# Moving evictions, waits and loads between engines at the borders of a two-layer graph transformer

## The chip, the cores and the metric

The kernel runs on one core of a Trainium2 chip. The metric is the device time of one execution in microseconds (us); the kernel before was run three times, with a median of 1898.72 us. One further execution was recorded by the hardware profiler, and all profile lines come from that one. Engines are named as the profile names them: PE is TensorE (matrix multiply), PEld its weight load, DVE is VectorE, ACT is ScalarE, POOL is GpSimd, SP is SyncE. SP, ACT and POOL each have a queue from which DMAs are issued, in the order in which the program lists them; an engine carries out its own instructions in order too.

## The reference

Two identical layers of a graph transformer over N = 2708 tokens of width 512, with 8 heads of 64:

```
mask   = adj + eye(n)
q,k,v  = h @ Wq.T + bq,  h @ Wk.T + bk,  h @ Wv.T + bv
scores = q.k / sqrt(64), -1e9 where mask == 0
ctx    = softmax(scores) @ v                       (per head)
h1     = layer_norm(h + ctx @ Wo.T + bo)
h2     = layer_norm(h1 + relu(h1 @ W1.T + b1) @ W2.T + b2)   (hidden width 2048)
```

The adjacency matrix `adj` is 2708 x 2708 int32 with a few ones in each row, so that attention is a sum over a handful of neighbours.

## The kernel before

All arithmetic is in 32-bit floats. Tokens are cut into 22 tiles of 128 rows (`NT` = 22; the last has 20). The order of the work on every engine is the order in which the Python program emits it, written out by hand; the framework adds only the waits.

**Keys stage, layer 0** (`first`). For each tile `t`, PE makes the keys `k` (four matmul steps into a PSUM tile of tag "g", three buffers) and the values `v` (tag "f", three buffers). DVE adds the key bias and evicts `k` into `kvs` (L919); ACT evicts `v` (L921); ACT's queue then issues the write of the tile before into DRAM (`kv_d`, L923). Beside this `lists(t)` turns rows of the adjacency into a list of neighbours: SP's queue loads 128 rows of `adj` into `aj` (1354 KB, two buffers, L691), POOL adds the diagonal (L692), ACT writes a code of each entry (L696, two `code` buffers), and DVE finds the largest entries by MAX8 (L699, L703, L706). `LEAD` sets how many lists have been emitted at a tile: `while done < min(NT, 1 + LEAD * t)`. With `LEAD` = 1.3 the last list is emitted at t = 16. `counted()`, some 35 DVE instructions on how long the lists are, is emitted at the start of t = 21. `matrix(w, "Wq", ...)` is loaded by POOL's queue at t = `QT` = 6. `beside_keys` loads layer weights at t = 17, 20 and 21.

**Queries stage, layer 0** (`first_queries`). Each of 22 tiles is projected to `q` (tags "g" and "f" in turn). At t = 1 `ranked` sorts the tokens by the length of their lists (PE, then DVE); at t = 3 `inverted` makes `ident_i`, the order of the tokens, with which every later gather is addressed, and `last_keys` evicts the last tile's keys. At t = `OWN` = 7 PE turns three gathered tiles `xr`.

**Attention** (`attend`) is a generator: one step handles up to two neighbours of each of 128 tokens. POOL gathers their rows (L1068), DVE multiplies and reduces (L1105, L1111), ACT takes the exponential and weighs (L1124, L1131), DVE adds (L1137, L1144). `advance(x)` runs steps by a credit of x; `through(k)` runs all that block `k` still needs. The end of a tile's attention is `cx` (L1175).

**Blocks.** `attended` turns `cx`, fetches the residual rows `xb` (in layer 0 a gather by POOL, in layer 1 a load by SP), projects with Wo and normalises to `h`. `feed_forward` runs over f = 0 to 15 for each of 11 blocks of two tiles: `pf` (L1440), relu on ACT (L1451), second product `a` (L1413). In it, at f = 10 (12 for the very first block), the next block's `attended` begins.

**Border to layer 1.** `Layer.query` makes the queries of layer 1, evicts them on DVE (L1346), and `kept` writes them to `q_d` by SP's queue (L1357). Eight tiles' inputs are preloaded (`pool`); `queries` streams the others through three `zT` buffers, loaded by SP (L1332). `keys_values` turns the last block (ACT copies `zT`) and makes its keys and values.

```
            for _ in streamed:
                if len(got) < 2:
                    advance(0.6)
            through(0)
            early[n] = now.attended(blocks[0], got)
```

Of the kernel before, what the change touches and what calls it, by code (L numbers as in the profile page):

```python
# [18 lines left out]
P = 128  # L19
# [25 lines left out]
LEAD = 1.3  # L45
QT = 6
# [433 lines left out]
def by_edges(ctx: ExitStack, tc: tile.TileContext, x, xT, adj, layers, out, redo):  # L480
# [134 lines left out]
    def lists_of(pa):  # L615
# [69 lines left out]
        def lists(t):  # L685

            q0, r = t * P, size(t)
            aj = pa.tile([P, N], I32, tag="aj", name="aj")
            if len(full) > 1:
                kept()  # L690
            nc.sync.dma_start(out=aj[:r], in_=adj[q0 : q0 + r, :])  # L691
            nc.gpsimd.tensor_tensor(  # L692
                aj[:r, q0 : q0 + r], aj[:r, q0 : q0 + r], diag[:r, :r], ALU.add
            )
            code = codes[t % 2]
            nc.scalar.activation(halves(code, BF16, 1)[:r], aj[:r], AF.Square)  # L696
            tops = pa.tile([P, len(parts), 8], F32, tag="tops", name="tops", bufs=3)
            for k, (m, mw) in enumerate(parts):
                nc.vector.max(out=tops[:r, k, :], in_=code[:r, m : m + mw])  # L699
            full.append((t, tops))  # L700
            left = tops.rearrange("p k e -> p (k e)")
            for k in range(0, LIST, 8):
                nc.vector.max(out=top[:r, t, k : k + 8], in_=left[:r])  # L703
                if k + 8 < LIST:
                    cb = pa.tile([P, len(parts) * 8], F32, tag="cb", name="cb")
                    nc.vector.match_replace(  # L706
                        out=cb[:r],
                        in_to_replace=top[:r, t, k : k + 8],
                        in_values=left[:r],
                        imm_value=0.0,  # L710
                    )
                    left = cb
# [153 lines left out]
    def first(w, meanwhile):  # L866
# [41 lines left out]
        for t in range(NT):  # L908
            r = size(t)
            if t == NT - 1:  # L910
                counts = counted()
# [6 lines left out]
            if t < NT - 1:  # L918
                nc.vector.tensor_tensor(kv[:r, :DM], k[:r], bk[:r], ALU.add)  # L919
# [7 lines left out]
            while done < min(NT, 1 + LEAD * t):  # L927
                lists(done)
                done += 1
            meanwhile(t)  # L930
# [11 lines left out]
    def first_queries(bq, wq, counts, placing, pa, tokens, last_keys, meanwhile):  # L942
# [22 lines left out]
        for t in range(NT):  # L965
# [7 lines left out]
            if t == 3:  # L973
# [276 lines left out]
    class Layer:  # L1250
# [102 lines left out]
        def kept(self):  # L1353
            if self.due:
                g, qs = self.due
                r = size(g)
                nc.sync.dma_start(out=q_d[self.n][g * P : g * P + r, :], in_=qs[:r])  # L1357
            self.due = None

        def attended(self, block, got):  # L1360

            cTs, hs = [], []
            for g in block:
# [4 lines left out]
                xb = dn.tile([P, DM], F32, tag="row", name="xb", bufs=3)  # L1368
                fetch(self.n, xb, x if self.n == 0 else xb_d[self.n], g)
                cTs.append((g, r, cT, xb))  # L1370
            yield
            for g, r, cT, xb in cTs:
# [225 lines left out]
    def beside_keys(t):  # L1598

        if t == NT - 5:  # L1600
            now.load_first()
        if t > NT - 3:
            now.load_second(t + 2 - NT, temp)
            now.load_w1(t + 2 - NT, nc.gpsimd if t == NT - 2 else nc.sync)
            now.load_w2(t + 2 - NT)

    def beside_queries(t):

        if t < 2:
            now.load_w1(t + 2, nc.scalar)  # L1610
            now.load_w2(t + 2, nc.scalar)
# [19 lines left out]
    for n in range(NL):  # L1631
        last = n == NL - 1
        nxt = None if last else Layer(n + 1, layers[n + 1])
        if n > 0:
# [7 lines left out]
            while pool:  # L1642
                advance(0.6)
                now.query(*pool.pop(0))
            for _ in streamed:
                if len(got) < 2:
                    advance(0.6)
# [7 lines left out]
            finish(streamed)  # L1655
# [4 lines left out]
        turning = projecting = None  # L1660
        for k, block in enumerate(blocks):
# [4 lines left out]
            for f, zs in enumerate(now.feed_forward(block, hs, hT)):  # L1666
                if f == NFC:
                    break
                if f in (5, 6, 7, 8) and behind:
                    next(behind)  # L1670
                if more and f == 10 + 2 * (k + n == 0):
                    through(k + 1)
                    projecting = now.attended(blocks[k + 1], got)
# [122 lines left out]
```

## Time and profile before

| | |
|---|---|
| median of 3 runs | 1898.72 us (1898.07 to 1901.28) |
| profiled execution, its own time | 1895.18 us |
| its span, first to last instruction | 1893.4 us |
| PE busy | 1841.4 us, 97% |
| DVE busy | 1390.7 us, 73% |
| ACT busy | 932.1 us, 49% |
| POOL busy | 744.9 us, 39% |
| HBM traffic | 314.79 MB read, 50.65 MB written |

The span is what the trace covers; 1.8 us lie around it. Times inside the trace count from the span's start. PE being busy nearly throughout, time can only come from the places where it waits, or runs at half of its clock; these are few, and the stage in which each one lies matters more than the shares of the whole.

### The profile page before, as it was taken

The page shows a single profiled execution, that of the slowest core. Times are in us where ns is not written, and L with a number is a line of the kernel's source. Part 1 is how long each engine was busy: PE and PEld are TensorE (multiplying, and loading weights), DVE is VectorE, ACT ScalarE, POOL GpSimd, SP SyncE. Part 2 cuts the span into 40 slices and gives each one's busy share as a digit, 9 for nine tenths or more (in the row PEclk, how much of TensorE's full clock was granted, in tenths as well). Part 3 has the DMA queues.
Part 4 walks back from the last instruction along what each step waited for, and adds up shares of the span by engine and source line. Part 5 has one row for each costly group of instructions (what it writes and reads, how often), then busy time and mean ns, then how long its engine had stood idle before and what let it go on. Part 6 is the DMA issues. An engine that isn't in the chain of part 4 may idle for free. (4 is left out here: it accounts for less than half of the span.)

```text
span 1893.4 us, 20835 instructions
## 1 busy us (share of the span) xinstructions
PE 1841.4 (97%) x6172; PEld 1091.3 (58%) x6172; DVE 1390.7 (73%) x2181; ACT 932.1 (49%) x3218; POOL 744.9 (39%) x714
## 2 busy tenths in 40 slices
PE   8999999999999999999999998999999999999996
PEld 4434455665666656666565643566666666666663
DVE  6897668877777858678684165789898898888931
ACT  4651335555445555455543122556565575566520
POOL 2111655434444434434431041435454556355210
PEclk9999999999999999999999999999999999999998
DMA  8999967546545555553531775836454765465200
GB/s 314 348 314 289 356 208 239 194 145 228 178 158 170 172 195 172 183 184 118 194 134 52 252 276 202 288 119 238 161 198 164 244 228 179 145 217 189 84 11 9
DMA packets 133019, 366.91 MB, mean 194 GB/s; under 512 B 19290, under 2 KB 39082, under 8 KB 130188
## 3 DMA queue, kind: packets, MB, share of 16 engines
q0 software_dynamic: 69600, 248.45, 38.3%
q1 hardware_dynamic: 51652, 97.04, 15.0%
q10 hardware_dynamic: 11644, 20.00, 2.9%
q8 instruction: 50, 0.82, 0.2%
q14 instruction: 73, 0.60, 0.1%
HBM read 314.79 MB, written 50.65 MB: 193 GB/s over the span
## 5 line engine op out<-in xcount | busy, mean ns | idle before, releaser
L1440 PE MATMUL pf<-hT,w 128*128 128x256 f32 (+1 forms) x2816 | 632.8, 372 | 6.2 <-ACT hT L1246 4.6
L1440 PEld LDWEIGHTS pf<-hT,w 128*128 128x128 f32 x2816 | 518.4, 190 | 179.8 <-issue 98.0
L1068 POOL DMA_INDIRECT kv<-kv_d,listed x420 | 503.7, 1199 | 300.4 <-DVE acc L1144 126.6
L1413 PE MATMUL a<-w,ft 128*128 128x512 f32 x1312 | 611.1, 592 | 0.0
L1451 ACT ACTIVATE ft<-pf,b 128x256 f32<-128x256 f32 (+1 forms) x336 | 154.6, 462 | 452.8 <-PE pf L1440 437.0
L1413 PEld LDWEIGHTS a<-w,ft 128*128 128x128 f32 x1312 | 246.8, 190 | 187.4 <-issue 170.4
L1131 ACT ACTIVATE kv<-kv,p 128x64 f32<-128x64 f32 x1232 | 311.0, 335 | 5.0
L1231 POOL TENSOR_TENSOR rd<-va,mhalf 128x1 f32<-128x1 f32 (+1 forms) x88 | 81.2, 923 | 555.3 <-DVE va L1229 555.3
L1105 DVE TENSOR_TENSOR kv<-kv,q 128x1024 f32<-128x1024 f32 (+1 forms) x222 | 256.6, 1156 | 17.8 <-DMA q<-q_d,ident_i 11.5
L1111 DVE TENSOR_REDUCE sc<-kv 128x16 f32<-128x1024 f32 (+1 forms) x222 | 257.9, 1162 | 7.6
L1144 DVE TENSOR_TENSOR acc<-acc,kv 128x1024 f32<-128x1024 f32 (+2 forms) x178 | 205.2, 1153 | 68.3 <-ACT kv L1131 53.9
L1124 ACT ACTIVATE p<-sc,listed 128x8 f32<-128x8 f32 x420 | 103.7, 296 | 117.9 <-DVE sc L1111 87.0
L1137 DVE TENSOR_TENSOR kv<-kv,p 128x512 f32<-128x512 f32 (+1 forms) x178 | 122.8, 690 | 42.1 <-ACT p L1124 37.8
L587 PE MATMUL o<-wo,cT 128*128 128x512 f32 x336 | 148.1, 593 | 0.0
L587 PEld LDWEIGHTS o<-wo,cT 128*128 128x128 f32 x336 | 63.5, 190 | 80.9 <-issue 75.6
L1175 ACT ACTIVATE cx<-acc,su 128x64 f32<-128x64 f32 (+1 forms) x352 | 88.3, 333 | 18.2 <-issue 7.2
L696 ACT ACTIVATE code<-aj 128x2708 bf16<-128x2708 int32 (+1 forms) x22 | 73.2, 3327 | 48.0 <-POOL aj L692 48.0
L1235 DVE SCALAR_TENSOR_TENSOR h<-h,rd,ln_b 128x512 f32<-128x512 f32 (+1 forms) x88 | 66.1, 751 | 39.9 <-POOL rd L1231 39.9
L587 PE MATMUL k<-wk,xg 128*128 128x512 f32 x168 | 82.4, 636 | 12.0 <-DVE kvs L919 7.0
L699 DVE MAX8 tops<-code 128x8 f32<-128x247 f32 (+2 forms) x242 | 78.7, 400 | 17.8 <-ACT code L696 17.6
L1375 DVE TENSOR_TENSOR h<-o,xb 128x512 f32<-128x512 f32 (+1 forms) x44 | 30.2, 686 | 83.6 <-PE o L587 32.6
L1131 ACT ACTIVATE acc<-kv,p 128x64 f32<-128x64 f32 (+1 forms) x352 | 88.8, 334 | 1.4
(168 smaller groups left out, 1502.4 us busy)
## 6 DMA issues: line engine op xcount, KB each, us to landing
aj<-in_adj SPq DMA_DIRECT2D x21, 1354.0 KB
kv_d<-kvs ACTq DMA_DIRECT2D x21, 512.0 KB
xg<-in_xT SPq DMA_DIRECT2D x19, 512.0 KB
w<-in_W SPq DMA_DIRECT2D x19, 512.0 KB
kv<-kv_d,listed POOLq DMA_INDIRECT x420
w<-in_W ACTq DMA_DIRECT2D x12, 512.0 KB
q_d<-qs SPq DMA_DIRECT2D x22, 256.0 KB
zT_d<-zT SPq DMA_DIRECT2D x22, 256.0 KB
```

The source lines that it names most:

```text
L587: nc.tensor.matmul(o[:r], xs(c), wm[:, c, :], start=(c == 0), stop=(c == NC - 1))
L1068: return nc.gpsimd.indirect_dma_start(out=to, out_offset=None, in_=table[:, :], in_offset=bass.IndirectOffsetOnAxis(ap=s, axis=0), bounds_ ...
L1105: nc.vector.tensor_tensor(kv[:r, :c, :DM], kv[:r, :c, :DM], self.q[:r].unsqueeze(1).to_broadcast([r, c, DM]), ALU.mult,)
L1111: nc.vector.tensor_reduce(self.sc[:r, s0 : s0 + c, :], kv[:r, :c, :DM].rearrange("p s (h d) -> p s h d", d=DK), AX.X, ALU.add,)
L1124: nc.scalar.activation(p[:r, s, :], self.sc[:r, s, :], AF.Exp, bias=minus[:r, g, s : s + 1])
L1131: nc.scalar.activation(to[:, i, hd], kv[:r, i, DM + h * DK : DM + (h + 1) * DK], AF.Copy, scale=p[:r, s0 + i, h : h + 1],)
L1137: nc.vector.tensor_tensor(to[:, 0, :].rearrange("p (h d) -> p h d", d=DK), kv[:r, 0, DM:].rearrange("p (h d) -> p h d", d=DK), p[:r, s0, : ...
L1144: nc.vector.tensor_tensor(self.acc[:r, :c, :], self.acc[:r, :c, :], kv[:r, :c, DM:], ALU.add)
L1175: nc.scalar.activation(cx[:r, hd], self.acc[:r, 0, hd], AF.Copy, scale=self.su[:r, h : h + 1])
L1413: nc.tensor.matmul(a[:r], fts[f][:, c0 : c0 + r], self.w2[f // 2][:, f % 2, :], start=(f == 0), stop=(f == NFC - 1),)
L1440: nc.tensor.matmul(pf[:, :w], self.w1[f // 2][:, c, f % 2 * P : f % 2 * P + P], hT[:, c, :w], start=(c == 0), stop=(c == NC - 1),)
L1451: nc.scalar.activation(ft[:, :w], pf[:, :w], AF.Relu, bias=self.b1[:, f : f + 1])
```

## The change

The keys of tiles 0 to 20 are copied out of PSUM by ACT, and POOL then adds the bias in SBUF. Rows of `adj` are loaded, coded and released in two halves (four buffers of half the size, so the same memory). `LEAD` falls to 1.2, which emits the last list at t = 17, and `counted()` follows it directly. Wq is loaded at t = 16, the first layer weights at t = 19. Four pairs of W1 and W2 pieces are loaded by POOL's queue, where before one W1 piece was; two pairs came from ACT's queue. `inverted` and `last_keys` move from t = 3 to t = 4. In layer 0, the residual rows of the next block are gathered at f = 5 (7 in the first block), ahead of `attended`. In layer 1's opening the queries are written by ACT's queue (while `apart` holds), the attention steps are emitted at other places and with a credit of 0.65.

```diff
@@ -42,8 +42,8 @@
 CXB = 3
 AHEAD = 10
 XB, XBS = 256, 11
-LEAD = 1.3
-QT = 6
+LEAD = 1.2
+QT = 16
 OWN = 7
 LISTS = (6, 9, 11, 14, 15, 17, 18, 19, 20, 21)
 EARLY = 3
@@ -685,15 +685,23 @@
         def lists(t):
 
             q0, r = t * P, size(t)
-            aj = pa.tile([P, N], I32, tag="aj", name="aj")
             if len(full) > 1:
                 kept()
-            nc.sync.dma_start(out=aj[:r], in_=adj[q0 : q0 + r, :])
-            nc.gpsimd.tensor_tensor(
-                aj[:r, q0 : q0 + r], aj[:r, q0 : q0 + r], diag[:r, :r], ALU.add
-            )
             code = codes[t % 2]
-            nc.scalar.activation(halves(code, BF16, 1)[:r], aj[:r], AF.Square)
+            for n0, n1 in ((0, N // 2), (N // 2, N)):
+                aj = pa.tile([P, N - N // 2], I32, tag="aj", name="aj", bufs=4)
+                nc.sync.dma_start(out=aj[:r, : n1 - n0], in_=adj[q0 : q0 + r, n0:n1])
+                d0, d1 = max(q0, n0), min(q0 + r, n1)
+                if d0 < d1:
+                    nc.gpsimd.tensor_tensor(
+                        aj[:r, d0 - n0 : d1 - n0],
+                        aj[:r, d0 - n0 : d1 - n0],
+                        diag[:r, d0 - q0 : d1 - q0],
+                        ALU.add,
+                    )
+                nc.scalar.activation(
+                    halves(code, BF16, 1)[:r, n0:n1], aj[:r, : n1 - n0], AF.Square
+                )
             tops = pa.tile([P, len(parts), 8], F32, tag="tops", name="tops", bufs=3)
             for k, (m, mw) in enumerate(parts):
                 nc.vector.max(out=tops[:r, k, :], in_=code[:r, m : m + mw])
@@ -907,8 +915,6 @@
         done, before = 0, None
         for t in range(NT):
             r = size(t)
-            if t == NT - 1:
-                counts = counted()
             xs = tokens(t, 0)
             kv = wts.tile([P, 2 * DM], F32, tag=f"w2_{5 + t % 3}", name="kvs")
             k = project(xs, r, wk, "k")
@@ -916,7 +922,8 @@
                 finish(turning)
                 finish(turning_q)
             if t < NT - 1:
-                nc.vector.tensor_tensor(kv[:r, :DM], k[:r], bk[:r], ALU.add)
+                nc.scalar.copy(kv[:r, :DM], k[:r])
+                nc.gpsimd.tensor_tensor(kv[:r, :DM], kv[:r, :DM], bk[:r], ALU.add)
             v = project(xs, r, wv, "v", other=True)
             nc.scalar.copy(kv[:r, DM:], v[:r])
             if before:
@@ -927,6 +934,8 @@
             while done < min(NT, 1 + LEAD * t):
                 lists(done)
                 done += 1
+                if done == NT:
+                    counts = counted()
             meanwhile(t)
             if t == QT:
                 wq = matrix(w, "Wq", "wq", nc.gpsimd)
@@ -970,7 +979,7 @@
             if t == 1:
                 parts = ranked(*counts)
                 evicted(0, held, qs)
-            if t == 3:
+            if t == 4:
                 inverted(parts)
                 last_keys()
                 pa.__exit__(None, None, None)
@@ -1354,10 +1363,20 @@
             if self.due:
                 g, qs = self.due
                 r = size(g)
-                nc.sync.dma_start(out=q_d[self.n][g * P : g * P + r, :], in_=qs[:r])
+                by = nc.scalar if self.apart else nc.sync
+                by.dma_start(out=q_d[self.n][g * P : g * P + r, :], in_=qs[:r])
             self.due = None
 
-        def attended(self, block, got):
+        def residuals(self, block):
+
+            xbs = []
+            for g in block:
+                xb = dn.tile([P, DM], F32, tag="row", name="xb", bufs=3)
+                fetch(self.n, xb, x if self.n == 0 else xb_d[self.n], g)
+                xbs.append(xb)
+            return xbs
+
+        def attended(self, block, got, xbs=None):
 
             cTs, hs = [], []
             for g in block:
@@ -1365,11 +1384,10 @@
                 cx = got.pop(g)
                 cT = dn.tile([P, NC, P], F32, tag="cT", name="cT", bufs=3)
                 flip(cx, r, cT[:, :, :r], self.bv)
-                xb = dn.tile([P, DM], F32, tag="row", name="xb", bufs=3)
-                fetch(self.n, xb, x if self.n == 0 else xb_d[self.n], g)
-                cTs.append((g, r, cT, xb))
+                cTs.append((g, r, cT))
+            xbs = xbs or self.residuals(block)
             yield
-            for g, r, cT, xb in cTs:
+            for (g, r, cT), xb in zip(cTs, xbs):
                 o = project(lambda c: cT[:, c, :r], r, self.wo, "o")
                 h = dn.tile([P, DM], F32, tag="h", name="h", bufs=4)
                 nc.vector.tensor_tensor(h[:r], o[:r], xb[:r], ALU.add)
@@ -1597,18 +1615,18 @@
 
     def beside_keys(t):
 
-        if t == NT - 5:
+        if t == NT - 3:
             now.load_first()
         if t > NT - 3:
             now.load_second(t + 2 - NT, temp)
-            now.load_w1(t + 2 - NT, nc.gpsimd if t == NT - 2 else nc.sync)
-            now.load_w2(t + 2 - NT)
+            now.load_w1(t + 2 - NT, nc.gpsimd)
+            now.load_w2(t + 2 - NT, nc.gpsimd)
 
     def beside_queries(t):
 
         if t < 2:
-            now.load_w1(t + 2, nc.scalar)
-            now.load_w2(t + 2, nc.scalar)
+            now.load_w1(t + 2, nc.gpsimd)
+            now.load_w2(t + 2, nc.gpsimd)
         if t == 6:
             now.settle()
             now.load_w1(4, nc.scalar)
@@ -1640,11 +1658,12 @@
             next(ahead)
             next(streamed)
             while pool:
-                advance(0.6)
+                if len(pool) < 3:
+                    advance(0.65)
                 now.query(*pool.pop(0))
-            for _ in streamed:
-                if len(got) < 2:
-                    advance(0.6)
+            for i, _ in enumerate(streamed):
+                if len(got) < 2 or i < 6:
+                    advance(0.65)
             through(0)
             early[n] = now.attended(blocks[0], got)
             next(early[n])
@@ -1652,12 +1671,14 @@
             next(streamed)
             for _ in blocks[0]:
                 next(early[n])
-            finish(streamed)
+            for i, _ in enumerate(streamed):
+                if i < 3:
+                    advance(0.6)
             now.apart = False
             now.load_w2(NFC // 2 - 1)
         *_, hs = early[n]
         hT = now.turned(blocks[0], hs)
-        turning = projecting = None
+        turning = projecting = xbs = None
         for k, block in enumerate(blocks):
             more = k + 1 < NB
             asking = iter(())
@@ -1668,9 +1689,12 @@
                     break
                 if f in (5, 6, 7, 8) and behind:
                     next(behind)
+                if more and n == 0 and f == 5 + 2 * (k == 0):
+                    xbs = now.residuals(blocks[k + 1])
                 if more and f == 10 + 2 * (k + n == 0):
                     through(k + 1)
-                    projecting = now.attended(blocks[k + 1], got)
+                    projecting = now.attended(blocks[k + 1], got, xbs)
+                    xbs = None
                     next(projecting)
                 if more and f == 11 + 2 * (k + n == 0):
                     *_, hs_next = projecting
```

## What was predicted

> **What bounds the kernel now.** First the page's busy times and slices.
>
> ```profile
> PE 1841.4 (97%) x6172; PEld 1091.3 (58%) x6172; DVE 1390.7 (73%) x2181; ACT 932.1 (49%) x3218; POOL 744.9 (39%) x714
> ...
> PE   8999999999999999999999998999999999999996
> ...
> DMA  8999967546545555553531775836454765465200
> ```
>
> PE works nearly throughout, so only its gaps can be won. The first slices (keys) and those after 1100 us (border to layer 1) have full DMA queues. Second, PE's waits, longest first (total us, times, longest):
>
> ```profile
> PE k L587 <- DVE kvs L919: 7.0, 3, 3.9
> PE q L587 <- DMA zT<-zT_d: 7.0, 1, 7.0
> ...
> PE tp L1241 <- ACT cx L1175: 4.7, 3, 4.4
> ...
> PE tp L1241 <- DVE h L1235: 3.4, 2, 2.9
> ```
>
> Each is a place that this change touches: keys waiting for eviction, queries for their input, the next block for attention, and for its h. Third, the stretches around them (length, busy us and count of each engine, clock, DMA share, GB/s), and PE in order of time:
>
> ```profile
> 85.00:100.00 15.00, 12.34 (x26) 5.15 (x25) 13.18 (x48) 9.55 (x5) 1.89 (x6) 0.89 0.96 343
> ...
> 138.00:151.00 13.00, 9.15 (x18) 3.72 (x17) 11.83 (x42) 7.48 (x4) 3.96 (x9) 0.87 1.00 283
> ...
> 1139.00:1150.00 11.00, 4.03 (x6) 1.51 (x5) 10.11 (x14) 6.34 (x26) 0.00 (x0) 0.73 0.89 351
> ...
> 1227.00:1238.00 11.00, 6.39 (x21) 4.00 (x19) 10.76 (x14) 10.39 (x43) 2.72 (x2) 0.84 0.49 178
> ```
>
> ```profile
> 142.93 5.40 PE L587 MATMUL k<-wk,xg 128*128 128x512 f32 x8 [3.85 <-DVE kvs L919]
> ```
>
> A gap costs more than its wait: the eight matmuls behind this one took 5.40 us, elsewhere 3.60, since the granted clock fell. DVE is busy 11.83 of 13 us there: it is late with lists, and the keys' eviction stands behind them in its order.
>
> **The change, part by part.**
>
> *Keys by ACT and POOL, LEAD, halves.* Rows:
>
> ```profile
> L919 DVE TENSOR_TENSOR kvs<-k,bk 128x512 f32<-128x512 f32 x21 | 14.0, 672 | 6.0 <-PE k L587 6.0
> ...
> L692 POOL TENSOR_TENSOR aj<-aj,diag 128x128 int32<-128x128 int32 x21 | 9.5, 453 | 92.5 <-DMA aj<-in_adj 88.9 <-ACT kvs L921 3.6
> ...
> L692 POOL TENSOR_TENSOR aj<-aj,diag 20x20 int32<-20x20 int32 x1 | 0.2, 214 | 2.8 <-DMA aj<-in_adj 2.8
> ```
>
> DVE loses 21 x 0.67 = 14 us. ACT gains 21 copies at 0.56 (its copy of v) = 12 us, and the second start of 22 codes: a 2708-wide one takes 3.33 us, a 64-wide activation 0.33, so halves are some 1.8 us each, +0.26 a list, 6 us. By its two L692 shapes POOL pays 2.2 ns a column, so 1.3 us for 512, 27 us in all. The Trainium skill ("GPSIMD Engine Reference", Engine selection) speaks against this: two-input elementwise work belongs on VectorE, GpSimd being about half as fast. Taken as a chain, 0.56 + 1.3 - 0.67 = 1.2 us a tile would make it 25 us slower. I take the trace: POOL was busy 9.21 of the 72 us from 13 to 85, and only the write to DRAM, issued a tile later on ACT's queue, waits for the bias. Behind the bias on POOL stand the next list's diagonal and tops; their `aj` lands later than the key (POOL waited 91.7 us for it in all), so nobody is kept.
>
> What PE waits for is now ACT, which stands in order behind the codes, and these behind `aj`. Codes came every 6.0 us (the first began at 18.7, the last at 144.07, 21 between). With LEAD 1.2 list 21 belongs to t = 17. At the old pace its code ends near 147, and the key of tile 18 is evicted right behind it. Its buffer is wanted by tile 21: a tile takes PE 16 x 0.43 = 6.87 us, tile 1 began at 16.75, so tile 21 at 154. 7 us remain. DMA descriptors halve from 10832 to 5416 bytes: the trace's 10832-byte ones took 37.6 ns a KB, 4096-byte ones 38.8, so at most 3% (nearest row), 20% at its 1024-byte row. Early freeing pulls the other way. I take nothing. Then all waits for kvs go: 2.67 + 0.53 + 3.85 at 88, 118 and 143 us, and twice 5.40 - 3.60 of slow clock: **-10.7 us**.
>
> *Counting sooner* runs on a DVE with no key eviction waiting: nothing; it costs 9.5 us (162.8 to 172.2) that ended just ahead of its use and now end some 5 us ahead. *Wq at t = 16* is wanted at t = 22, 40 us on; *first weights at t = 19* a stage later; their four POOL issues (0.54 each) and five small SP ones leave the place where SP's queue held `aj` and `xg` loads, if anything a gain. *Weights by POOL*: seven more issues at 0.5 to 0.8 us, about 5 us, at 150 to 160 us, where POOL was nearly idle and the DMA queues had a hole (0.71 over 151:167). They leave SP and ACT queues that waited for nothing critical. Without that cover they'd delay the index gathers by up to 5 us; I take zero.
>
> *`inverted` one tile later.* Two costs. It takes its five POOL gathers and the last kv_d write along. `k` of the last tile now holds a "g" buffer while q of t = 4 wants one, so that it waits for q of t = 0, evicted behind `ranked`. From the first `ranked` matmul to that eviction took 9.8 us (174.24 to 184.04); PE's work between is 1.8 + 2 x 3.44: +1.2 us. Then only three queries, not four, lie between `ident_i` and the turning of `xr`. The third `xr` landed 14.1 us after `ident_i` (185.6 to 199.7) and cost a 1.0 us wait; with 3.44 us less cover: +2.6 (none if its transfer meets less traffic; 1.8 more if the clock falls, as it did behind waits of 2.67, 3.85, 6.97 and 4.40, not behind one of 2.9). Sum **+3.8 us**.
>
> *Residual rows sooner.* At 313 us two gathers were issued, and DVE waited 6.5 us for the first; then PE waited 2.9 for `h` and 0.6 for the copies behind. Five f-steps of 3.44 us earlier the 8 us transfer is covered: **-3.3 us** (idle PE in 327:338). The other waits for `xb` cost DVE only. In POOL's order two issues of 1.0 us now stand before some key gathers, once a block; the "row" buffers they take are free at f = 5, `turned_row` having ended at f = 4. Past the first block DVE has that slack: PE had no wait for it from 338 to 700.
>
> *Queries written by ACT.* The 7.0 us wait had its load issued at 1138.01, behind two writes that waited for DVE; the buffer had been free since 1132.6. From issue to landing it took 8.4 us, so it now lands at 1141 against a need at 1139.4: of 9.4 us (7.0, and 2.4 at the lower clock) 1.6 stay. But the same line puts the last two writes of layer 0 ahead of ACT's copies of the last block's zT: these started at 1098.79, the second query's eviction ended at 1100.27, plus an issue of 0.33: +1.9. Each later write makes ACT wait for an eviction that DVE does ahead of the scores which ACT's next exponential needs, so it adds nothing there (0.33 us an issue). Net **-5.9 us**. Attention allows it: with rows landing at 1121.8 + 1.9, six steps of 4.3 us (1.22 + 1.22 + 0.68 + 1.22) and ten evictions of 0.69 end at 1156.4, and PE, at 1108.5 + 1.9 + 14 x 3.44 + 1.6, asks at 1160; before it did at 1166.0.
>
> *Attention moved at the border.* Idle DVE time at 1166:1190 (10.86 busy of 24) takes about two steps, as the three new advances of 0.6 ask for: 8.6 us of lead for block 1, with their gathers at POOL, which issued only 8 in that stretch. The wait for cx at 1227 was 4.4, with slow clock 5.7: **-5.7 us**. If the lead isn't there it stays.
>
> Sum: -10.7 + 3.8 - 3.3 - 5.9 - 5.7 = -21.8. The profiled execution took 1895.18, span 1893.4, so 1873.4 for its like; the median of runs stands 3.5 higher, so 1877.
>
> **The rivals.**
>
> *A: attention sets the border.* PE arrives earlier, finds the same gathers (DMA share 1.02 over 1117:1147) and waits as long, in the first block or in a later one. DVE busy 434.65 of 500 us over 1250:1750 speaks for it, its idle time at 1166 against it. Without the last two gains: 1889.
>
> *B: slower; ACT becomes the bound of the keys.* One late half stops ACT, and with it keys, values and their writes. The 7 us of margin are gone at 6.36 us a list; beyond, each 0.1 us costs 2.1 us at the last list. Slower than before needs 22 us more, that is 7.4 us a list, DMA descriptors 23% dearer per byte. For it: DMA is 0.92 to 1.00 full, halves start off a row's boundary, ACT now carries 2 x 0.56 + 0.33 + 1.2 x 3.6 = 5.8 of each 6.87 us. Against: the 4096-byte row. At 7.7: 1905.
>
> *C: the change doesn't do what it says.* Lists are paced by DMA; PE finishes keys early and gives it back waiting for `ident_i`, and the border's loads stay late. Then 1898, no change. Against it: list 21 was coded at 147, yet counting started at 162.8, behind evictions.
>
> **How the numbers follow.** My case 0.60 (1867 to 1884: 9 less if the flips and border cost nothing, 7 more with the clock's fall and one step missing); A 0.20; B 0.14; C 0.06. The measurement tells 0.2%, 3.8 us, from no change. Faster is my case and A, 0.80; same 0.06; slower 0.14. The range leaves out B and the tail: 1866 to 1894.
>
> **What would show it.** Right: no PE wait for kvs, queries starting near 156.5 instead of 167.3; a wait of 3 to 4 us for xr near 189; no wait for h near 320; zT's wait under 2 us; no wait for cx in the first block of layer 1. Wrong: PE's k or v waiting for ACT's kvs, codes further apart than 6.3 us, the half-clock stretches returning, or DVE waiting for the kv gathers at the border.

## The result, and the profile after

The changed kernel takes 1873.12 us in the median (1872.13 to 1875.34, 4 runs), the kernel before in the same series 1899.72 (1898.07 to 1901.28, 4 runs): a ratio of 0.9862 [0.9845, 0.9879], 26.6 us less. The profiled executions are 1895.18 and 1872.77 us, 22.4 apart; what follows explains these 22.4.

The page of the kernel after, busy time, PE's slices and the DMA engines' slices:

```profile
PE 1834.5 (98%) x6172; PEld 1090.1 (58%) x6172; DVE 1378.4 (74%) x2160; ACT 941.9 (50%) x3261; POOL 778.7 (42%) x743
...
PE   8999899999999999999999999999999999999997
...
DMA  9999867646545455463541676836554664446300
```

DVE and ACT moved as the diff says: 21 fewer DVE instructions, 43 more on ACT (21 copies, 22 second halves). PE is 7 us less busy with the same 6172 matmuls, because fewer of them ran at half clock.

PE's waits in the kernel after (total us, times, longest):

```profile
PE tp L1250 <- DMA xr<-in_x,ident_i: 7.9, 2, 6.5
PE pf L1458 <- ACT hT L1255: 6.3, 4, 2.2
...
PE q L587 <- DMA zT<-zT_d: 1.8, 2, 1.4
PE k L582 <- ACT zT L1255: 1.3, 1, 1.3
PE q L587 <- DVE qs L959: 1.0, 1, 1.0
PE o L587 <- ACT cT L1255: 1.0, 1, 1.0
...
PE tp L1250 <- DVE h L1244: 0.6, 1, 0.6
```

The waits for `kvs` (7.0 us) and for `cx` (4.7) are gone, those for `zT` (7.0) and `h` (3.4) have shrunk to 1.8 and 0.6. Three came new: `qs` 1.0 and ACT's `zT` copies 1.3, foreseen in kind, and ACT's copies of `cT` 1.0, not foreseen. One grew beyond what was foreseen: PE now waits 7.9 us for `xr`, for which it waited 0.8 before:

```profile
PE tp L1241 <- DMA xr<-in_x,ident_i: 0.8, 1, 0.8
```

Three stretches of the kernel after (length, then busy us and count of PE, PEld, DVE, ACT, POOL, then clock, DMA share, GB/s). The first two are those of before, in the keys; the third is the turning of `xr`:

```profile
85.00:100.00 15.00, 15.00 (x37) 6.63 (x36) 11.40 (x41) 11.42 (x10) 3.33 (x7) 1.00 1.01 388
138.00:151.00 13.00, 13.00 (x32) 5.74 (x31) 12.09 (x49) 2.34 (x4) 5.61 (x8) 1.00 0.75 219
185.00:198.00 13.00, 5.12 (x17) 3.14 (x17) 2.77 (x6) 1.76 (x3) 10.19 (x10) 0.66 1.01 357
```

In the keys PE is full and at full clock, 13.00 of 13 us with 32 matmuls where 9.15 us with 18 stood before. DVE is nearly as full with its lists as it was (12.09 of 13 us in the second stretch), but PE no longer waits for it. In the third stretch PE works 5.12 of 13 us at a mean clock of 0.66, and the DMA engines are full.

Where the time went is best seen by following marks on PE, one start time after the other. The last column is what the prediction booked for the part since the mark above.

| mark on PE (or the end) | before | after | shift | since the mark above | predicted |
|---|---|---|---|---|---|
| queries start | 167.27 | 154.61 | -12.7 | -12.7 | -10.7 |
| own queries, behind the turning of `xr` | 200.27 | 196.97 | -3.3 | +9.4 | +3.8 |
| layer 0, first `pf` of block 0 | 267.11 | 264.64 | -2.5 | +0.8 | 0 |
| layer 0, first `pf` of block 1 | 336.50 | 330.43 | -6.1 | -3.6 | -3.3 |
| layer 1, first query | 1091.18 | 1084.16 | -7.0 | -0.9 | 0 |
| layer 1, first `pf` of block 0 | 1189.83 | 1179.65 | -10.2 | -3.2 | -5.9 |
| layer 1, first `pf` of block 1 | 1265.23 | 1248.96 | -16.3 | -6.1 | -5.7 |
| last matmul | 1875.63 | 1861.15 | -14.5 | +1.8 | 0 |
| end of the span | 1893.39 | 1871.04 | -22.3 | -7.9 | 0 |

Up to the last matmul the change won 14.5 us, not 21.8. The other 7.9 came behind it, where nothing was predicted. The total landed near the forecast because these two misses offset each other, which is luck.

Each column is one execution. In a second profiled execution of the changed kernel (`after_again` below) the own queries came +7.3 where this one has +9.4, the first `pf` of block 0 +1.9 (here +0.8), that of block 0 in layer 1 -1.7 (here -3.2); every other row agreed within 0.2 us. So those three rows are known to some 2 us, not to 0.1.

The end can be seen in the timeline. The last instruction that the kernel after has on POOL starts 5.25 us ahead of its end, that of the kernel before started at 1880.26, 13.1 us ahead of its end:

```profile
1865.79 1.05 POOL L1040 DMA_INDIRECT out<-h,ident_i  x1 [1.09 <-DVE h L1244]
```

What lies between is the drain of POOL that closes the program: 9.298 us in the records of the trace before, 1.867 after, with the same last DMA. By the trace's records of DMA packets its last packet is done 2.45 us after the issue begins before and 2.46 after, and in both the drain begins only then, so its length is no wait for these packets. The other queues wait for it, as SP's own waits at the program's end show (total, times, longest), before:

```profile
SPq L1792 <- PEq L1792: 9.5, 2, 8.6
```

and after:

```profile
SPq L1816 <- PEq L1816: 1.6, 2, 1.1
```

The other miss, `xr`, comes from farther back. The DMA issues of the kernel after (queue, count, KB each, median us from issue to landing):

```profile
w<-in_W POOLq DMA_DIRECT2D x8, 512.0 KB, 16.0
...
rec_d<-rec ACTq DMA_DIRECT2D x1, 504.0 KB, 27.2
```

And what POOL waited for from 170 to 200 us, before and after:

```profile
POOL listed L1068 <- DVE ident_i L862: 32.7, 1, 32.7
```

```profile
POOL listed L1077 <- DMA rec_d<-rec: 25.7, 1, 25.7
```

`rec_d` is written in two pieces: 504 KB (L811), then the last 20 records, 3.8 KB (L815). The issue of the second, before and after (duration in ns, start):

```profile
L807 ACTq DMA_DIRECT2D rec_d<-rec x1: 8050/8050/8050, 173.5 to 173.5; - x1
```

```profile
L815 ACTq DMA_DIRECT2D rec_d<-rec x1: 19414/19414/19414, 157.5 to 157.5; - x1
```

`rec_d` holds the records from which POOL gathers the lists in `inverted`, ahead of the rows for `xr`. It is written when counting is done, now at 155.2 us; just then POOL's queue issues 4 MB of weights (151.7 to 157.7 us). The 504 KB take 27.2 us to land. The small write behind them holds ACT's queue for 19.4 us in its issue alone. By the trace's packets the last of `rec_d` is through 26.4 us after the first issue, at 181.7; before, it was 10.9 us, at 183.1, ahead of `ident_i` at 185.6. So now the first list is gathered at 183.4 although `ident_i` was ready at 176.2, and the `xr` gathers behind are late by as much.

### The profile page after: what moved, and what is told of

It reads as the page before. It is cut to its first block, busy times and chain, and to the rows that moved or that the text cites. A ratio compares the mean times of both kernels' runs of the same rounds, so it can differ in the third digit from the quotient of the medians.

```text
span 1871.0 us, 20950 instructions
## 1 busy us (share of the span) xinstructions
PE 1834.5 (98%) x6172; PEld 1090.1 (58%) x6172; DVE 1378.4 (74%) x2160; ACT 941.9 (50%) x3261; POOL 778.7 (42%) x743
## 4 chain that ended last, share of the span: by engine, by line
PE 86%; DVE 5%; DMA 4%; ACT 2%; issue 2%; POOL 0%; SPq 0%; ACTq 0%; POOLq 0%; DVEq 0%
PE pf L1458 29%; PE a L1431 28%; PE k L587 8%; PE v L587 8%; PE o L587 7%; PE q L587 3%; PE tp L1250 2%; DVE kv L1114 1%; DMA rec_d<-rec 1%; DVE sc L1120 1%; ACT kv L1140 1%; DVE kv L1146 1%; DMA w<-in_W 1%; PE a L1446 1%; ACT cx L1184 1%
## 5 line engine op out<-in xcount | busy, mean ns | idle before, releaser
L1114 DVE TENSOR_TENSOR kv<-kv,q 128x1024 f32<-128x1024 f32 (+1 forms) x222 | 256.7, 1157 | 12.7 <-DMA q<-q_d,ident_i 11.6
L587 PE MATMUL k<-wk,xg 128*128 128x512 f32 x168 | 77.1, 602 | 5.1 <-DMA wk<-in_Wk 5.1
L1518 ACT COPY kvs<-v 128x512 f32<-128x512 f32 (+1 forms) x22 | 12.9, 586 | 132.9 <-PE v L587 131.9
```

Source lines behind the costliest of these rows:

```text
L587: nc.tensor.matmul(o[:r], xs(c), wm[:, c, :], start=(c == 0), stop=(c == NC - 1))
L1114: nc.vector.tensor_tensor(kv[:r, :c, :DM], kv[:r, :c, :DM], self.q[:r].unsqueeze(1).to_broadcast([r, c, DM]), ALU.mult,)
```

## The experiments

Times in brackets are the range of the runs. "Own queries" and "last matmul" are marks of the table above, as shifts against the kernel before; "tail" is the time from the last matmul's start to the end of the span.

**The changed kernel once more.** No edit.

> The changed kernel once more, as the reference of this call. About 1873 us against 1899 of before, ratio 0.986. It is also to show whether what lies behind PE's last matmul is steady: in the profile of the changed kernel 9.9 us lay there, before 17.8, and the difference was one wait of POOL at its last drain (1.87 against 9.30). If that belongs to the change, this profile has the short one again; if it varies by execution, it need not.

1874.96 us (1871.45 to 1882.71), ratio 0.9887 [0.9867, 0.9907]. Last matmul -14.0, tail 9.9 us, drain 1.867 as in the first trace: the short drain belongs to the kernel, not to one execution. PE's gain is again 14 us, short of 21.8. The wait for `xr` is 5.6 us here, not 7.9; in the four kernels below that leave the weights, Wq and `inverted` alone (`border_back`, `lead_back`, `halves_back`, `kept_sp`) it is 5.9 to 7.2. Two of the six runs took 1882 us; they were not profiled, and why is open.

**Weights back on SP's and ACT's queues** (`pairs_back`).

```diff
-            now.load_w1(t + 2 - NT, nc.gpsimd)
-            now.load_w2(t + 2 - NT, nc.gpsimd)
+            now.load_w1(t + 2 - NT, nc.gpsimd if t == NT - 2 else nc.sync)
+            now.load_w2(t + 2 - NT)
...
-            now.load_w1(t + 2, nc.gpsimd)
-            now.load_w2(t + 2, nc.gpsimd)
+            now.load_w1(t + 2, nc.scalar)
+            now.load_w2(t + 2, nc.scalar)
```

> The changed kernel with the four early weight pairs issued as before (SP and ACT, one piece by POOL). Theory: the 4 MB that POOL issues within 6 us share the DMA engines with the write of rec_d, which goes in pieces of 192 bytes, and the first index gather waits for that write (at 183.4 us, though ident_i is there at 176.1). Then here the first index gather starts within 1 us of ident_i, the wait for xr falls from 8.4 us (of 7.9 counted) to 1 to 4, and the kernel is 4 to 6 us faster than the changed one: 1868. Rival: rec_d is slow by its own small pieces, whatever flows beside it; then the gather starts at 183 again and the time stays at 1873. Second rival: the loads moved to POOL were themselves needed there; then the first feed-forward block waits and it is slower, 1876 or more.

1873.96 us (1870.72 to 1877.27), 0.9865 [0.9846, 0.9884]: the same time as the whole change, by another road. The four runs lie in two pairs, at 1870.7 and 1877.2; the profiled one is of the upper pair. The write of `rec_d` is issued later, at 165.8 in place of 155.2, though the records were ready at 154.3: ACT's own weight loads (163.1 and 163.9) now stand ahead of it. It is through sooner, 12.7 us after its issue in place of 26.4, at 178.5 in place of 181.7:

```profile
L815 ACTq DMA_DIRECT2D rec_d<-rec x1: 8261/8261/8261, 166.2 to 166.2; - x1
```

The first list is gathered at 180.0, PE stands idle 2.8 us at `xr` in place of 7.9 (5.6 in `after_again`), own queries stand at -8.2 and the last matmul at -17.6. But the drain is 9.298 us again and the tail 17.3, and in SP's waits at the end:

```profile
SPq L1816 <- PEq L1816: 9.0, 2, 8.5
```

So the weights on POOL's queue cost PE 3 to 5 us at `xr`, and gave 7.4 back at the very end. This edit moves the loads to other queues and also spreads them, from 6 us to 27 us (148.6 to 175.9); whether the queue or the crowding slowed `rec_d` is not separated by it.

**Only the keys' evictions** (`keys_only`: the kernel before with them).

```diff
-                nc.vector.tensor_tensor(kv[:r, :DM], k[:r], bk[:r], ALU.add)
+                nc.scalar.copy(kv[:r, :DM], k[:r])
+                nc.gpsimd.tensor_tensor(kv[:r, :DM], kv[:r, :DM], bk[:r], ALU.add)
```

> The kernel before with one edit: keys of tiles 0 to 20 evicted by ACT, bias by POOL. Theory: the eviction behind DVE's lists was the whole cause of the waits at 88, 118 and 143 us, so all three vanish, the queries start 10 to 12 us sooner (155 to 157 us) and the time falls by as much: 1888. Rival: without the slower lists (LEAD 1.2), the halves and the later Wq, ACT stands behind the codes and PE waits for ACT instead: queries start at 160 or later and the time is 1893 or more.

1892.34 us (1889.73 to 1895.0), 0.9966 [0.9954, 0.9979], 6.2 us below the kernel before in the same series. Queries start 5.3 us sooner, not 12.7; the last matmul stands at -2.5. PE's waits in this kernel:

```profile
PE k L587 <- ACT kvs L919: 5.0, 2, 3.7
```

The wait has only changed its name: DVE's eviction stood behind DVE's lists, now ACT's stands behind ACT's codes. The eviction's move alone isn't the gain of the keys.

**Layer 1 opened as before** (`border_back`: in the changed kernel, the three loops that hand out attention steps and the queue of the `q_d` write).

```diff
-                by = nc.scalar if self.apart else nc.sync
-                by.dma_start(out=q_d[self.n][g * P : g * P + r, :], in_=qs[:r])
+                nc.sync.dma_start(out=q_d[self.n][g * P : g * P + r, :], in_=qs[:r])
...
-                if len(pool) < 3:
-                    advance(0.65)
+                advance(0.6)
...
-            for i, _ in enumerate(streamed):
-                if len(got) < 2 or i < 6:
-                    advance(0.65)
+            for _ in streamed:
+                if len(got) < 2:
+                    advance(0.6)
...
-            for i, _ in enumerate(streamed):
-                if i < 3:
-                    advance(0.6)
+            finish(streamed)
```

> The changed kernel with layer 1's opening as before: queries written by SP, attention steps at the old places and credits. Theory: the wait for zT (about 9 us with its slow clock) and the wait for cx in the first block (about 6) come back, less what writing by ACT cost (1.5): by the marks of PE in the two profiles 3.2 and 6.1 us, so 1882. Rival: attention sets the border, and the earlier stages' gain shifts all of it; then 1873 to 1875.

1881.1 us (1878.83 to 1883.44), 0.9912 [0.9897, 0.9927]. Both waits are back, in the places where they were (the first is the one for `zT`: PE waited for the semaphore of that load, and the profile names the DVE instruction that ended last):

```profile
PE q L587 <- DVE kv L1114: 7.5, 1, 7.5
...
PE tp L1250 <- ACT cx L1184: 4.6, 2, 4.4
```

The last matmul stands at -8.3, 6.1 us worse than with the change, and the median is 6.1 above that of `after_again` in the same series. Counted from the first query of layer 1 the border's edits are worth 7.8 us to PE (+0.3 here, -7.5 with the change), while 11.6 were predicted.

**Only the weights on POOL** (`pairs_only`: the kernel before with the eight loads by `nc.gpsimd`, the edit of `pairs_back` the other way).

> The kernel before with one edit: the four early weight pairs issued by POOL (eight DMAs, where before POOL issued one of them). Theory: POOL's last drain is short (1.87 us) in every kernel that issues these eight on POOL, and 9.30 in every one that does not, so here it is 1.87 and the tail 7.4 us shorter; on PE's side the later write of rec_d costs 0 to 5 us at the xr turning. Time 1892 to 1897. Rival: the short drain comes from another part of the change (halves, evictions, order), then it is 9.30 here and the time 1898 to 1903.

1892.05 us (1887.68 to 1897.82, 12 runs), 0.9967 [0.9954, 0.9981]. SP's waits at the end:

```profile
SPq L1792 <- PEq L1792: 2.0, 2, 1.4
```

The drain is 1.867 us and the tail 10.2. A kernel with nothing but other queues for its weights is faster, and in its profiled execution PE is not: its last matmul stands at +7.3. The write of `rec_d` is not slowed: it is issued at 176.3, 15.6 us after the last of the eight loads, and is through in 7.6 us; PE waits 0.8 us for `xr`, as before. So in these runs the loads on POOL's queue did harm only where the write of `rec_d` came right behind them. Four of the 7.3 us lie in the keys, whose code is the same: PE's waits for `kvs` there were 10.7 us, as against 7.0. So a part of +7.3 is the spread of that stage from execution to execution, and the price of these loads on PE is read from `pairs_back`.

**The same queue, later weights** (`pairs_later`: `pairs_back`, and in block 0; all six loads so moved fall in layer 0, at 270 to 279 us).

```diff
                 if k == 0 and len(now.w1) < NFC // 2 and f % 2 == 0:
-                    now.load_w1(len(now.w1), nc.scalar)
-                    now.load_w2(len(now.w2), nc.scalar)
+                    now.load_w1(len(now.w1), nc.gpsimd)
+                    now.load_w2(len(now.w2), nc.gpsimd)
```

> The changed kernel with the four early weight pairs back on SP and ACT, and the three pairs of the first feed-forward block (six DMAs, about 80 us later) issued by POOL in place of ACT. Theory: the drain depends on how many DMAs POOL issues in all, not on which (545 here, 546 in the changed kernel, 539 before), so it is 1.87 again, and rec_d is written as soon as in pairs_back: 1873.5 less 7.4, 1866 to 1867, faster than both kernels. Rival 1: the drain stays 9.30, so it is 1874. Rival 2: the loads hold POOL's gathers back in the first block, PE waits there for 2 us or more, and 1869 or above.

1864.88 us (1863.85 to 1866.39), 0.9827 [0.9809, 0.9844]: 8.2 us below the changed kernel by the medians, some 6.6 by the two ratios, and 6.7 by the profiled spans. The intervals of the ratios just miss each other (the change's begins at 0.9845). PE's waits and SP's at the end:

```profile
PE tp L1250 <- DMA xr<-in_x,ident_i: 2.0, 1, 2.0
...
PE q L587 <- DVE qs L959: 1.0, 1, 1.0
```

```profile
SPq L1816 <- PEq L1816: 1.7, 2, 1.2
```

It has the short drain (1.703) and the quick write of `rec_d` (through 11.9 us after its issue, at 177.1): the first list is gathered at 178.7, own queries stand at -9.3 and the last matmul at -21.1. Both halves of the reading are shown at once, by moving loads that nothing waits for. Not all of the 6.7 us is `xr`: 2 us come in block 0 of layer 0, where PE's wait of 1.0 us for ACT's `ft` is gone now that ACT issues no loads there, and 1 to 2.6 (against the two executions of the change) are lost again ahead of block 0 of layer 1.

**`LEAD` as before** (`lead_back`).

```diff
-LEAD = 1.2
+LEAD = 1.3
```

> The changed kernel with LEAD 1.3 in place of 1.2. Theory: the later lists are what keeps ACT's codes from holding the keys, the rest of what keys_only lacked; PE waits for ACT's kvs at about 111 and 133 us again, queries start near 160 in place of 154.6. As only 60% of a shift there reached the end in keys_only, 1876 to 1879. Rival: halves (freed sooner, started sooner) do it; then no wait, 1874.

1873.22 us (1872.6 to 1874.09), 0.9871 [0.9854, 0.9889]. Queries start at 154.5, and no wait for `kvs` is in PE's list. Alone, `LEAD` is indifferent.

**Whole rows of `adj`** (`halves_back`).

```diff
-            for n0, n1 in ((0, N // 2), (N // 2, N)):
-                aj = pa.tile([P, N - N // 2], I32, tag="aj", name="aj", bufs=4)
...
+            aj = pa.tile([P, N], I32, tag="aj", name="aj")
+            nc.sync.dma_start(out=aj[:r], in_=adj[q0 : q0 + r, :])
...
+            nc.scalar.activation(halves(code, BF16, 1)[:r], aj[:r], AF.Square)
```

> The changed kernel with whole rows of the adjacency (one load, one code, two buffers). Theory: the halves are near neutral; codes come every 6 us as before, queries start within 1 us of 154.6, time within 2 us of 1874. Rival: halves carry the keys stage; queries start at 158 or later, 1877 or more.

1874.79 us (1873.63 to 1879.19), 0.9878 [0.9861, 0.9896]. No wait for `kvs`, queries start at 155.26. Its profiled execution (1879.19 us) has a wait that the changed kernel doesn't show:

```profile
PE pr L789 <- DVE before L761: 4.1, 1, 4.1
```

Lists end later with whole rows, so DVE's counting is late for `ranked`. In the median it costs nothing that these runs can tell.

**Wq and the first weights at their old places** (`wq_back`).

```diff
-QT = 16
+QT = 6
...
-        if t == NT - 3:
+        if t == NT - 5:
             now.load_first()
```

> The changed kernel with Wq loaded at t = 6 and the first layer weights at t = 17, as before. LEAD and whole rows, put back singly, brought no wait for kvs; keys_only, which lacked both and this, had two. Theory: the 1 MB of Wq in the thick of the adjacency loads is what makes ACT late, then PE waits for kvs at 110 to 135 us, queries start 2 us or more after 154.6. Rival: it takes two of the three together; then no wait, start within 1 us, and time within 2 us of 1873.

1868.57 us (1866.62 to 1872.57), 0.9852 [0.9829, 0.9874]; beside it the kernel before took 1897.43. Queries start at 155.59 without a wait for `kvs`, so this was not what freed the keys either. Its median lies 4.5 us below that of the change, though the two intervals overlap. What it does better in its profiled execution is seen in PE's waits:

```profile
PE tp L1250 <- DMA xr<-in_x,ident_i: 2.6, 1, 2.6
```

The first list is gathered at 179.5 and the last matmul stands at -19.7. The write of `rec_d` is through 21.8 us after its issue, against 26.4 and 24.8 in the two executions of the change. That it meets less traffic because Wq and the first weights were loaded earlier is an inference from this; no run separates Wq from the first weights.

**Queries written by SP** (`kept_sp`: of the border's edits only the queue).

```diff
-                by = nc.scalar if self.apart else nc.sync
-                by.dma_start(out=q_d[self.n][g * P : g * P + r, :], in_=qs[:r])
+                nc.sync.dma_start(out=q_d[self.n][g * P : g * P + r, :], in_=qs[:r])
```

> The changed kernel with the queries of layer 1 written by SP, as before, and the new places of the attention steps. Theory: the zT loads stand behind those writes again; the wait for zT grows from 1.6 to 6 us or more with a slow clock behind, and the wait of 1.5 us for ACT's zT copies at 1092 goes; by these PE's last matmul comes 5 us later, time 1878. Rival: the steps alone are enough, since the first two preloaded queries no longer wait behind gathers: zT's wait stays under 3 us and the time is 1873 or less.

1872.38 us (1871.07 to 1873.51), 0.9868 [0.9849, 0.9888]. PE's waits from 1080 to 1270 us:

```profile
PE q L587 <- DMA zT<-zT_d: 3.3, 1, 3.3
PE pf L1457 <- ACT hT L1255: 1.1, 1, 1.1
```

The wait for `zT` is 3.3 us, not 7: the steps' new places have already removed more than half of it. The waits for ACT's `zT` copies and for `cT` are gone, and `hT` is back at 1.1. From the first query to block 0 this kernel wins 4.4 us over before. The change wins 3.2, and 1.7 in `after_again`; 2.5 to 3.9 us are won by the other four kernels with the same border and the same loads in block 0. The last matmul stands at -16.2, 1.7 better than the change. Over whole runs the two can't be told apart.

**One load more** (`one_more_pool`: the kernel before, the W1 piece of t = 21 by POOL too; one run).

```diff
-            now.load_w1(t + 2 - NT, nc.gpsimd if t == NT - 2 else nc.sync)
+            now.load_w1(t + 2 - NT, nc.gpsimd)
```

> The kernel before with the second early W1 piece issued by POOL too: 540 DMAs by POOL, where before it issued 539. If the short last drain comes at some count between 539 and 545 this may show 9.30 or 1.7 to 1.9; either narrows the place. If the drain followed from the load of one certain piece, it would be 1.87.

1898.55 us, drain 9.543. That piece is not the one that shortens the drain; see below.

**Later weights, and `inverted` at its old place** (`pairs_later_inv3`: `pairs_later`, and this).

```diff
-            if t == 4:
+            if t == 3:
                 inverted(parts)
```

> pairs_later with inverted and last_keys back at t = 3. Theory: the wait of 1.2 us of the fourth query for a PSUM buffer goes, a wait of about 0.7 for the table takes its place, ident_i comes 3 us sooner and the four queries ahead of the xr turning cover its gathers: PE 2 to 3 us sooner there, time 1862 to 1863. Rival: rec_d's write (landing near 178) bounds the first gather, not ident_i; then nothing is won at xr, 1865.

1865.1 us (1864.44 to 1868.72), 0.9831 [0.9813, 0.9849]. `ident_i` is ready 4.1 us sooner (173.2), the first list is gathered only 2.6 sooner (176.1), since the last packet of `rec_d` is through at 174.0; own queries are 1.7 us better and the last matmul 1.0, at -22.1. The time is that of `pairs_later`: with the write of `rec_d` in the way, the tile's delay is worth 1 to 2 us on PE, and nothing that the runs can tell.

## Why the prediction was right, and where it was wrong

Time and direction were right, the time in part by luck: PE won 7.3 us less than the sum, and 7.9 us came from a place that the prediction left out. By its steps:

*Keys: right in mechanism and, within the spread, in size.* Predicted -10.7, measured -12.7, against one execution of the old stage; the end of that stage varied by 6 us between executions (last section). All waits for `kvs` and both stretches of slow clock went; about 1.5 us of the 12.7 lie in the first 10 us of the program, where the first eight matmuls took 5.22 us in place of 6.72, fewer of them at the slow clock, which nothing in the change explains. The parts were sized well: POOL's bias add 1.3 us predicted, 1.29 measured; half a row's code 1.8 predicted, 1.72 measured. In the groups of the kernel after (busy us, mean ns, idle time and its releasers):

```profile
L702 ACT ACTIVATE code<-aj 128x1354 bf16<-128x1354 int32 x42 | 69.6, 1720 | 8.6 <-POOL aj L696 6.0 <-DVE tops L707 1.5 <-DMA aj<-in_adj 1.1
...
L926 POOL TENSOR_TENSOR kvs<-kvs,bk 128x512 f32<-128x512 f32 x21 | 27.0, 1286 | 62.0 <-ACT kvs L925 52.7 <-issue 6.4 <-DVE bk L575 2.9
```

The second row is why the rule of the Trainium skill that the prediction weighed ("GPSIMD Engine Reference", Engine selection: elementwise work on VectorE) would have misled here. Its ratio of about two agrees with this trace, its consequence doesn't: an add of nearly twice DVE's 0.67 us (DVE read PSUM, POOL reads SBUF), on an engine that waits 52.7 us for its input, held up nothing that PE waited for. But the prediction gave the gain to `LEAD`, halves and eviction as one. `keys_only` shows that the eviction alone is worth some 5 to 6 us (5.3 at the start of the queries, 6.2 by the medians) and leaves a wait of 3.7; `lead_back`, `halves_back` and `wq_back` show that each of the three others can be taken away singly without a wait for `kvs`. What any two of them together are worth was not tried. So which of them frees the remaining half of the gain stays open. Rival B named this very place, ACT standing behind codes; it holds for `keys_only`, not for the whole.

*`inverted` one tile later: +9.4 measured in place of +3.8.* The first term was right: q of t = 4 waited 1.0 us for the buffer (1.2 predicted). The second, +2.6 for less cover at `xr`, measured +7.0 (7.9 against 0.8), with another 1.3 of slow clock in the turning itself. (By the working's own figures the second term would be +3.4: where there is a wait already, 3.44 us less cover lengthens it by as much.) But the cause of the excess is not the tile. With the weights back on their queues (`pairs_back`) the same stretch costs +3.3, close to the predicted 3.8, and `pairs_later_inv3` finds only 1 to 2 us in the tile itself.

*Weights by POOL: the step that failed.* "I take zero" named the hole in the DMA queues as cover and "up to 5 us" without it. The zero was wrong: the loads cost PE 3 to 5 us. The 5 us named for the other case come out only by luck, since the path was another. Not POOL's seven added issues delayed the gathers (5 us at a time when POOL waited for 25.7), but the 4 MB that they asked for slowed ACT's write of `rec_d`, on which the gathers wait: through after 26.4 us with them, after 12.7 without. The hole of 151:167 was the very place where counting, moved up by this change, puts that write. A hole seen in the trace before was taken as free after other parts had moved into it.

*Wq and first weights: zero or a gain predicted, perhaps some us lost.* In `wq_back` the last matmul stands at -19.7 rather than -14.5 and -14.0, with an `xr` wait of 2.6 us rather than 7.9 and 5.6. The medians, 4.5 us apart, point the same way, but their intervals overlap, so this is not shown. If it is real, it is partly the same microseconds as the weights', and the two don't add.

*Residual rows: right*, -3.3 predicted, -3.6 measured.

*Queries written by ACT: mis-sized, -3.2 (-1.7 in `after_again`) in place of -5.9.* The waits came as worked out: `zT` 1.8 us (1.6 predicted), ACT's copies 1.3 (1.9 predicted). The failing term is "it adds nothing there", said of each later write: on ACT the copies of `cT` (PE waited 1.0) and `hT` (2.2, before 1.1) came later too. `kept_sp` goes further: with the queue as before and the steps of attention moved, the stretch gains 4.4; with neither (`border_back`) it loses 0.4. The working booked the gain to the queue; the runs give it to the moved steps. Why these help, DVE being sooner with what SP's writes wait for, is read from the traces and not tested by itself.

*Attention at the border: right*, -5.7 predicted, -6.1 measured, no wait for `cx`. So rival A is out, and `border_back` brings both waits back. Together the two border terms gave 9.3 of 11.6. But behind block 1 the change loses 1.8 us again, with one more wait of 1.5 us for ACT's `hT` (at 1634.7). This loss stands in every profiled kernel with the new border and not in `border_back`, so it belongs to the border's price, and nothing was predicted for it. `border_back` also reached layer 1 1.6 us sooner than the change, which is why its last matmul loses only 6.1.

*The end: nothing predicted, -7.9.* The prediction added nothing behind the last matmul, because no instruction of the change lies there. `after_again`, `pairs_back`, `pairs_only` and `pairs_later` show that the length of the drain follows the loads put on POOL's queue some 1600 to 1700 us earlier. Without the shorter drain the change would stand near 1880.

## What to carry to other kernels

When one part of a change brings a small critical write forward, look for what another part issues in the same 20 us: here 4 MB of weights, which nobody waited for, held 504 KB of records, and moving the loads instead to a time with no such write won 7 to 8 us more. A wait for an engine is only removed when the engine that takes over isn't itself held up; an eviction moved from DVE, where it stood behind lists, to ACT, where it stood behind codes, kept a wait of 3.7 us. Read also what lies behind the last matmul: here it was a third of what the profiled execution gained.

## What the runs showed of the hardware that was not expected

The last drain of POOL is either long or short. With 539 DMAs issued by POOL in the program (the kernel before, `keys_only`, `pairs_back`) it is 9.298 us, with 540 (`one_more_pool`) 9.543; with 545 (`pairs_later` and its variant) 1.703, with 546 (the changed kernel, `pairs_only`) 1.867. Kernels with the same count have the same length to the nanosecond, the eight profiled executions with 546 (`after_again`, `border_back`, `lead_back`, `halves_back`, `wq_back` and `kept_sp` too) however else they differ. The final output DMA is the same in all, its packets done 2.4 to 2.5 us after issue. So the count, or something that goes with it, decides between 540 and 545. It is not one certain load: the six that `pairs_later` adds are others than those of the change. All added loads are of 512 KB, so the number of DMAs, their packets and their bytes are not separated, and the mechanism is open.

A write that follows a burst of loads waits for much of it: `rec_d`, 504 KB in pieces of 192 bytes, was through 12.7 us after its issue when the weights came by SP and ACT, and 26.4 us (24.8 in the second trace) when POOL's queue had issued 4 MB just before. A write of 3.8 KB behind it on the same queue held ACT's queue for 8.3 and 19.4 us in its issue. Whether the small pieces matter was not tried.

The keys as they were before do not run alike each time: queries started at 165.4, 167.3 and 171.3 us in three kernels (`one_more_pool`, the kernel before, `pairs_only`) whose keys were the same code. In the ten profiled executions with the stage's whole change, or all but one part of it, they started between 154.4 and 155.8.
